# Unread products in the idle places of TensorE, two values in places of their own, and one copy moved to ScalarE

## The chip, the cores and the metric

The kernel runs on one core of a Trainium2 chip. The metric is the device time of one execution in microseconds (us); the time before is 784.37 us, the median of three runs (783.34 to 786.42). The core's engines work side by side, each through its own queue of instructions in order: TensorE (PE, with its weight loads shown as PEld) multiplies matrices into PSUM, VectorE (DVE) and ScalarE (ACT) work element by element, GpSimd (POOL) too, and SyncE (SP) issues transfers.

## The reference

A Perceiver of two layers: 128 latent rows of 256 numbers (`x`) attend to 12544 context rows. Each layer is cross attention to the context, a recurrent attention and a mixture of experts, each added to `x` after a layer norm (the last layer's, which the change touches, are the lines below). All is float32.

```python
x = x + L0_xattn(layernorm(x), ctx_1024, mask, ...)
x = x + L0_attn(layernorm(x), ...)          # gated delta net
x = x + L0_ffn(layernorm(x), ...)           # best expert of 8
x = x + L1_xattn(layernorm(x), ctx_1024, ...)
x = x + L1_attn(layernorm(x), ...)          # here
x = x + L1_ffn(layernorm(x), ...)           # and here

# L1_attn: 16 heads of 16
q, k, v = split(x @ Wqkv.T)
q, k = elu(q) + 1, elu(k) + 1
decay = sigmoid(decay_param)                # one for each head
running_kv   = scan(k * v, decay)           # out[t] = decay * out[t-1] + in[t]
running_ksum = scan(k, decay)
den = clip(sum(q * running_ksum, per head), 1e-6)
out = q * running_kv / den
g = sigmoid(out @ Wgate.T + bgate)
return (g * out + (1 - g) * v) @ Wout.T

# L1_ffn: the two best of 8 experts
gate = softmax(x @ Wg + bg); keep the two largest, normalised
y = x @ We + be for every expert; sum over experts weighted by gate
```

## The kernel before

Until about 744 us the kernel streams the context: for each block of 512 rows it makes keys and values, then scores, exponentials and weighted sums, first for layer 0 and then for layer 1, with the layers between filled in. The end of that is `weigh1`: the last weighted sums (L1084), copies of the sums to SBUF by ScalarE (L1107), four transposes into the PSUM tile `pt` (L1110), the division (L1113, L1117), the residual (L1121), and a copy of the row totals, `total`, out of `pt` by ScalarE (L1123).

Then `last_layers` computes the second layer's recurrent attention and experts for all 128 rows at once, with nothing left to stream; its weights are in SBUF by then. Here the order of TensorE, ScalarE and VectorE is the order in which the code calls them (`tc.manual_schedule`), and only data that is not there yet, or a place that is still being read or written, makes an instruction wait. In this function the steps are:

- `root` (L1306 on): mean and variance of `x` (L1309, L1310), the inverse root by Ln and Exp on ScalarE (L1312, L1313), `x` less its mean (L1316).
- Layer norm and transposition in one product with a scaled identity, `dg` (L1325, L1329); the result `hT` is copied to SBUF in two halves, by VectorE (L1330) and ScalarE (L1331).
- Keys, queries and values, transposed, as `pk`, `pq`, `pv` (L1337, two halves of the channels, two products each), and the residual `x` started in `po` (L1341).
- exp and relu of keys and queries (L1346 to L1349) and a copy of `v` (L1350) on ScalarE, then a load of the table for sigmoid (L1351); `min(exp, 1) + relu` and the scan of the keys on VectorE (L1354, L1355), the queries' (L1356), and their product (L1357).
- Denominators: a product that sums per head (`pd`, L1361), clipped, inverted (L1366, L1367), spread to 256 columns (`dx`, L1369) and transposed (`pr`, L1372). TensorE adds `v` through the output weights to `po` (L1377) while VectorE scans keys times values (L1379), multiplies by the queries (L1380) and by `pr` to give `o` (L1382).
- The gate: four products of `o` (`pg`, L1386), sigmoid (L1390), and the table for Ln and Exp (L1393). Since g*o + (1-g)*v = v + g*(o-v), VectorE takes `o - v` (L1394), works out whether all totals are in range (L1398 to L1400), and multiplies by the gate (L1402); TensorE adds the result through the output weights to `po` (L1403).
- The layer norm again (its transposes L1414), the router's logits `pl` (L1421), the eight experts' products `py` (L1425, L1455), the choice of two on VectorE (L1433 to L1449), and the weighted sum of the experts into `y_out` (L1469, L1476), which is written out.

Intermediate values lie in places of the context's buffers that are free by then, handed out one after the other by `room` and `both`; in the profile they are all called `ctx`. [...]

A second copy of the network, for totals out of range, stands behind a branch that these inputs do not take.

## Time and profile before

| | |
|---|---|
| median of three runs | 784.37 us |
| profiled execution, its time | 784.51 us |
| its span, first to last instruction | 782.6 us |
| mean granted TensorE clock | 0.992 of full speed |
| TensorE busy in the span | 749.9 us (96%) |
| the span from 744 us on | 38.6 us, TensorE busy 23.3, granted clock 0.83 |
| last product of weigh1's sums, last sum into y_out | 745.3, 776.7 us |

How to read it: the granted clock is the share of full speed that TensorE was given in a stretch; a product of float32 operands shows as two rows or more of matmul, each with a weight load, and rows overlap, so the time that one adds is the distance from start to start rather than its own duration. In the timeline the brackets give the idle time of the engine ahead of an instruction, and what ended it.

### The profile page before, as it was taken

The numbers are of one execution on the slowest core, as the hardware profiler recorded it, in microseconds if no ns is written. First come the engines' busy times: TensorE is split into PE (matmuls) and PEld (weight loads), VectorE is DVE, ScalarE is ACT, GpSimd is POOL, SyncE is SP. The second block draws the span as 40 slices with busy tenths as digits, with TensorE's granted clock in tenths as the row PEclk, the third lists the DMA queues.
The fourth block names the chain that finished last, engine by engine and source line by source line (L and its number), as shares of the span: only waits on it lengthen the run. The fifth ranks groups of instructions, "written<-read, shape, count | busy, mean of one in ns | idle before, by whom it ended". The sixth has DMA issues, their size and how long they took to land.

```text
span 782.6 us, 23795 instructions
## 1 busy us (share of the span) xinstructions
PE 749.9 (96%) x10821; PEld 558.0 (71%) x10821; DVE 250.5 (32%) x406; ACT 411.2 (53%) x540; POOL 246.4 (31%) x193
## 2 busy tenths in 40 slices
PE   4999999999999999999999999999999999999965
PEld 2667777777777776756668756667888888888852
DVE  0465445654466453983113133000000000000044
ACT  2244334433443334474224533336999999999940
POOL 6597677666776630416012011000000000000000
PEclk9999999999999999999999999999999999999988
DMA  9584000000000002233111345221442222222000
GB/s 291 213 280 172 9 8 4 8 8 8 7 6 6 2 15 84 85 117 123 58 44 41 106 128 134 78 81 58 121 115 74 68 58 74 68 58 72 4 1 12
DMA packets 35742, 56.70 MB, mean 72 GB/s; under 512 B 5760, under 2 KB 11952, under 8 KB 35632
## 3 DMA queue, kind: packets, MB, share of 16 engines
q1 hardware_dynamic: 35232, 54.00, 21.7%
q8 instruction: 87, 1.43, 0.8%
q0 software_dynamic: 400, 1.09, 0.5%
q14 instruction: 23, 0.19, 0.1%
HBM read 42.09 MB, written 12.98 MB: 70 GB/s over the span
## 4 chain that ended last, share of the span: by engine, by line
PE 90%; DVE 3%; ACT 2%; POOL 1%; issue 1%; DMA 1%; SPq 0%; ACTq 0%; DVEq 0%; POOLq 0%
PE st L1067 14%; PE ot L1084 12%; PE pk L395 11%; PE pv L1016 10%; PE pv L408 10%; PE pk L995 10%; PE st L437 6%; PE ot L455 6%; DVE acc L612 1%; DMA ctx<-in_ctxT 1%; POOL shift L428 1%; PE pr L602 1%; PE py L924 1%; PE py L1425 1%; PE pg L732 1%
## 5 line engine op out<-in xcount | busy, mean ns | idle before, releaser
L1073 ACT ACTIVATE e<-st 128x512 f32<-128x512 f32 x196 | 189.7, 1021 | 17.1 <-PE st L1067 15.7
L428 POOL TENSOR_TENSOR shift<-mb,nm 128x1024 f32<-128x1024 f32 x49 | 120.7, 2464 | 73.7 <-DVE e L443 59.3
L1067 PE MATMUL st<-qs,ks 32*128 32x128 f32 x3136 | 115.8, 283 | 0.8 <-ACT e L1073 0.8
L1067 PEld LDWEIGHTS st<-qs,ks 32*128 32x128 f32 x3136 | 96.9, 186 | 21.4 <-ACT e L1073 20.9
L444 ACT ACTIVATE e<-e 128x1024 f32<-128x1024 f32 x49 | 51.8, 1057 | 101.5 <-DVE e L443 100.0
L1084 PE MATMUL ot<-e,ctx 128*17 128x128 f32 x3136 | 104.7, 274 | 0.0
L395 PE MATMUL pk<-ctx,wkv 128*128 128x512 f32 (+1 forms) x200 | 93.7, 613 | 9.3 <-DMA ctx<-in_ctxT 9.3
L443 DVE TENSOR_TENSOR e<-st,shift 128x1024 f32<-128x1024 f32 x49 | 57.9, 1220 | 113.5 <-PE st L437 105.2
L995 PE MATMUL pk<-ctx,wk 128*128 128x512 f32 (+1 forms) x200 | 92.8, 591 | 1.3 <-ACT ctx L1021 1.3
L1016 PE MATMUL pv<-wv,ctx 128*128 128x256 f32 x392 | 92.8, 382 | 0.9 <-ACT kh L1002 0.9
L408 PE MATMUL pv<-wkv,ctx 128*128 128x256 f32 x392 | 89.2, 380 | 1.6 <-ACT kT L399 1.6
L408 PEld LDWEIGHTS pv<-wkv,ctx 128*128 128x128 f32 x392 | 74.2, 190 | 22.3 <-issue 10.0
L445 DVE TENSOR_TENSOR sums<-sums,e 128x1024 f32<-128x1024 f32 x49 | 87.8, 1792 | 4.8 <-ACT e L444 1.2
L1016 PEld LDWEIGHTS pv<-wv,ctx 128*128 128x128 f32 x392 | 72.8, 190 | 20.4 <-issue 10.0
L1084 PEld LDWEIGHTS ot<-e,ctx 128*17 128x17 f32 x3136 | 77.5, 97 | 11.9 <-ACT e L1073 0.3
L423 POOL TENSOR_SCALAR mb<-msk 128x256 f32<-128x256 uint8 x49 | 72.2, 1474 | 4.2
L395 PEld LDWEIGHTS pk<-ctx,wkv 128*128 128x128 f32 x200 | 37.1, 195 | 48.4 <-issue 45.4
L1113 DVE RECIPROCAL den<-pt 128x16 f32<-128x16 f32 x1 | 0.3, 257 | 208.7 <-PE pt L1110 208.7
L1002 ACT ACTIVATE kh<-pk,col 128x512 f32<-128x512 f32 (+1 forms) x50 | 33.9, 678 | 59.0 <-PE pk L995 58.8
L995 PEld LDWEIGHTS pk<-ctx,wk 128*128 128x128 f32 x200 | 36.1, 190 | 31.5 <-issue 26.5
L1021 ACT COPY ctx<-pv 128x512 f32<-128x512 f32 x49 | 28.7, 587 | 54.3 <-PE pv L1016 54.2
L412 ACT COPY v<-pv 128x512 f32<-128x512 f32 x49 | 28.6, 586 | 54.3 <-PE pv L408 54.3
(322 smaller groups left out, 620.3 us busy)
## 6 DMA issues: line engine op xcount, KB each, us to landing
ctx<-in_ctxT SPq DMA_DIRECT2D x24, 512.0 KB, 8.4
kd<-kh SPq DMA_DIRECT2D x48, 256.0 KB, 2.0
ks<-kd SPq DMA_DIRECT2D x192, 64.0 KB, 2.8
w<-in_L_ffn_expert_w SPq DMA_DIRECT2D x4, 512.0 KB, 3.7
ctx<-in_L_ffn_We SPq DMA_DIRECT2D x4, 512.0 KB, 4.7
msk<-in_maskT SPq DMA_DIRECT2D x24, 64.0 KB, 1.9
w<-in_L_attn_Wqk SPq DMA_DIRECT2D x2, 768.0 KB, 9.7
w<-in_L_attn_Wv SPq DMA_DIRECT2D x2, 768.0 KB, 5.1
```

The lines of the kernel that those rows point to most:

```text
L395: nc.tensor.matmul(pk[:, :n], wkv[:, k, m * 128 : (m + 1) * 128], ctx_blocks[b][:, k, :], start=(k == 0), stop=(k == KC - 1),)
L408: nc.tensor.matmul(pv[:, c, :], ctx_blocks[b][:, k, rows], wkv[:, k, D:], start=(k == 0), stop=(k == KC - 1),)
L423: nc.gpsimd.tensor_scalar(mb, msk[:, c0 * 128 : (c0 + 2) * 128].rearrange("p (c s) -> p c s", c=2), BIG, BIG, ALU.mult, ALU.subtract,)
L428: nc.gpsimd.tensor_add(shift, mb.unsqueeze(1).to_broadcast([128, 4, 2, S]), nm.unsqueeze(2).to_broadcast([128, 4, 2, S]),)
L443: nc.vector.tensor_add(e, st, shift)
L444: nc.scalar.activation(e, e, AF.Exp)
L445: nc.vector.tensor_add(sums, sums, e)
L995: nc.tensor.matmul(pk, wk1[:, k, m * 128 : (m + 1) * 128], ctx_blocks[b][:, k, :], start=(k == 0), stop=(k == KC - 1),)
L1016: nc.tensor.matmul(pv[:, c, :], ctx_blocks[b][:, k, rows], wv1[:, k, :], start=(k == 0), stop=(k == KC - 1),)
L1067: nc.tensor.matmul(st3[:, j - 1, g, :] if j else st1[:, 0, g, :], kss[b % 3][r, g // 2, g % 2, c * 128 : (c + 1) * 128], qs[r, g, :], star ...
L1073: nc.scalar.activation(e[:, j].rearrange("p j g s -> p (j g s)"), st.rearrange("p j g s -> p (j g s)"), AF.Exp,)
L1084: nc.tensor.matmul(ot[32 * j : 32 * j + DH + 1, g, :], v[:, c, 8 * (g // 2) + 2 * j + g % 2, :], e[:, j, g, :], start=False, stop=(i + 1 = ...
```

## The change

Within `last_layers` and nowhere else:

- A PSUM tile `spare` in a bank of its own, taken from `tl_a`, which goes from three banks to two; and a function `beat(n)`, which issues `n` products of the identity with 256 columns of the first weights into `spare`. Nothing reads `spare`. It is called five times: 7 ahead of the first layer norm, 1 after the residual, 2 ahead of the transposes of the denominators, 2 after the gate's products, and 2 after the last products into `po`.
- The keys' two halves go to two PSUM tiles, `pk0` and `pk1`, in place of one; `tl_y` then has four users (`pk0`, `pk1`, `pq`, `pv`) for its four places.
- The copy that spreads the denominators, `dx`, goes from VectorE to ScalarE, and the load of sigmoid's table from ahead of it to behind it.
- `o - v` is written to a new place, `away`, in place of over `o`.

```diff
-            tc.tile_pool(name="tl_a", bufs=3, space=PSUM) as ps_a,
+            tc.tile_pool(name="tl_a", bufs=2, space=PSUM) as ps_a,
...
+            spare = ps_o.tile([128, 512], F32, name="spare")
+
+            def beat(n):
+
+                for _ in range(n):
+                    nc.tensor.matmul(spare[:, :D], ident, wqkv[:, 0, :D], start=True, stop=True)
...
             po = ps_o.tile([128, 512], F32, name="po")
+            beat(7)
             xm, y0, t = root(x)
...
-            pk, pq, pv = [wide(f"p{n}").rearrange("p j (k s) -> p j k s", s=S)[:, 0] for n in "kqv"]
-            for dst, n in ((pk, 1), (pq, 0), (pv, 2)):
+            pk = [wide(f"pk{m}")[:, 0, :S] for m in range(KC)]
+            pq, pv = [wide(f"p{n}").rearrange("p j (k s) -> p j k s", s=S)[:, 0] for n in "qv"]
+            for dst, n in ((pk, 1), ((pq[:, 0], pq[:, 1]), 0), ((pv[:, 0], pv[:, 1]), 2)):
...
-                            dst[:, m, :], wqkv[:, k, c : c + 128], hT[:, k, :],
+                            dst[m], wqkv[:, k, c : c + 128], hT[:, k, :],
...
             nc.tensor.matmul(po[:, :D], ident, x, start=True, stop=False)
+            beat(1)
...
-                nc.scalar.activation(ek[:, m, :], pk[:, m, :], AF.Exp)
-                nc.scalar.activation(rk[:, m, :], pk[:, m, :], AF.Relu)
+                nc.scalar.activation(ek[:, m, :], pk[m], AF.Exp)
+                nc.scalar.activation(rk[:, m, :], pk[m], AF.Relu)
...
             nc.scalar.copy(v, pv)
-            nc.scalar.preload_act_table_set("sigmoid_and_others")
...
-            nc.vector.tensor_copy(dx, den.unsqueeze(2).to_broadcast([S, 16, 16]))
+            nc.scalar.copy(dx, den.unsqueeze(2).to_broadcast([S, 16, 16]))
+            nc.scalar.preload_act_table_set("sigmoid_and_others")
+            beat(2)
...
             nc.scalar.preload_act_table_set("natural_log_exp_and_others")
-            nc.vector.tensor_sub(o, o, v)
+            beat(2)
+            away = both()
+            nc.vector.tensor_sub(away, o, v)
...
-                nc.vector.tensor_mul(gate[:, m, :], gate[:, m, :], o[:, m, :])
+                nc.vector.tensor_mul(gate[:, m, :], gate[:, m, :], away[:, m, :])
                 nc.tensor.matmul(po[:, :D], gate[:, m, :], wgo[:, m, D:], start=False, stop=(m == KC - 1))
             x = po[:, :D]
+            beat(2)
```

## The prediction

> **What bounds the kernel now.** First the page: what sets the end, by engine.

> ```profile
> PE 90%; DVE 3%; ACT 2%; POOL 1%; issue 1%; DMA 1%; SPq 0%; ACTq 0%; DVEq 0%; POOLq 0%
> ```

> TensorE sets the end for 90% of the span, but the change touches only the last layers, from 746.7 us on. So I read that stretch in windows (columns: PE, PEld, DVE, ACT, POOL busy, then granted clock, DMA share, GB/s).

> ```profile
> 740.00:744.00 4.00, 4.00 (x134) 3.60 (x130) 0.00 (x0) 3.67 (x5) 0.00 (x0) 1.00 0.00 0
> 748.00:751.00 3.00, 0.77 (x3) 0.80 (x4) 1.73 (x7) 0.50 (x2) 0.00 (x0) 0.72 0.00 0
> 752.00:753.00 1.00, 1.00 (x6) 1.00 (x6) 0.00 (x0) 0.00 (x0) 0.00 (x0) 0.50 0.00 0
> 757.00:758.00 1.00, 0.45 (x5) 0.35 (x4) 0.87 (x4) 0.98 (x1) 0.00 (x0) 1.00 0.00 0
> 767.00:768.00 1.00, 1.00 (x2) 0.45 (x2) 0.78 (x5) 0.02 (x1) 0.00 (x0) 0.50 0.00 0
> 770.00:772.00 2.00, 2.00 (x6) 0.95 (x5) 1.29 (x3) 0.00 (x0) 0.00 (x0) 1.00 0.00 0
> ```

> ```profile
> 42.80:46.22 3.41, 1.79 (x9) 1.00 0.25 38
> 745.95:749.36 3.41, 0.71 (x4) 0.99 0.00 0
> 749.36:752.78 3.41, 2.54 (x10) 0.50 0.00 0
> 759.60:763.02 3.41, 1.89 (x12) 1.00 0.00 0
> 763.02:766.43 3.41, 1.64 (x10) 0.99 0.00 0
> ```

> After 0.71 and 1.64 us of work the clock fell, after 1.79 and 1.89 it stayed; a half-clock period with 2.54 did not bring it back, a full one did. Then the timeline of that stretch for who waits for whom (start, duration, instruction, idle before and its releaser):

> ```profile
> 747.58 0.17 ACT L1123 COPY total<-pt 128x16 f32<-128x16 f32 x1 [1.40 <-DVE x_xattn L1117]
> 750.23 1.20 PE L1329 MATMUL ln_pt<-ctx 128*128 128x128 f32 x4 [3.56 <-DVE ctx L1325]
> 753.25 1.91 PE L1337 MATMUL pq<-ctx,w 128*128 128x128 f32 x8
> 757.98 0.29 DVE L1369 COPY ctx<-ctx 128x256 f32<-128x256 f32 x1
> 759.96 1.16 PE L1386 MATMUL pg<-ctx,w 128*128 128x128 f32 x8 [0.32 <-DVE ctx L1382]
> 761.15 0.43 DVE L1394 TENSOR_TENSOR ctx<-ctx,ctx 128x256 f32<-128x256 f32 x1 [1.25 <-PE pg L1386]
> 762.32 1.13 PE L1403 MATMUL po<-w,ctx 128*128 128x256 f32 x4 [1.20 <-DVE ctx L1402]
> 763.49 0.43 DVE L1309 BATCH_NORM_STATS2 ctx<-po 128x6 f32<-128x256 f32 x1 [1.02 <-PE po L1403]
> ```

> A product is two passes in these rows (L1377 has two products and four passes). Pass to pass, 128 columns take 0.11 us at full clock (pg) and 0.213 at half (pq); 256 columns take 0.217 (L1377, 1.03 for four) and so about 0.43 at half (py's 512 columns step 0.43 at full, 0.85 at half).

> **The change, part by part.** *Seven unread products at the head.* The spare bank is the one that pt had; the first product waits for the copy to total, which ends at 747.75. They run from 747.79: 14 passes x 0.217 = 3.04, to 750.83 at full clock. The real product, queued behind them on TensorE, could start at 750.23: 0.60 late. What this buys, if the clock holds: ln_pt's first result at 751.2, copy by VectorE 0.29, keys from 751.57 (751.38 before); 16 passes of keys and queries at 0.11, so pq is there at 753.50 (755.17 before). From pq to the denominators' product it takes 1.66 as now (ScalarE 0.68, VectorE 0.42 and 0.42, handoffs): 755.16 in place of 756.83. **Gain 1.7.** If it falls amid the seven, say at 748.5: 1.7 of them at full clock, then four until the next edge at 751.9, the rest by 752.5; keys from 753.2 at full clock, denominators at 756.75: gain 0.1. Bounds: 1.7 and, wholly at half clock, a loss (rival three). I take 1.7; the choice hangs on one period. The one that ended at 749.36 would hold 0.71 + 1.57 = 2.28 us, above the 1.79 that kept the clock. [...]

> *Keys' halves in places of their own.* ScalarE may start after four passes, not eight. At half clock queries end last anyway (scan done at 755.37, eq and rq at 755.87), gain 0. At full clock it keeps the second scan at 754.1, beside rq, where one tile would make it 754.4: contained in the 1.7. Four wide banks hold four users, and the narrow pool going from 3 to 2 adds no wait: each reused bank's reader (pd, pr, pg, ln_pt, pl) is already an ancestor of the next writer.

> *One unread product after po*: 0.43. At full clock TensorE ends pv at 754.21, po 754.64, this 755.07; the denominators' product is ready at 755.16. Hidden by 0.09; at half clock po and it would cost up to 1.6.

> *Spreading copy to ScalarE.* VectorE loses 0.295 + 0.02 before its scans. On ScalarE I take 0.38 (v's copy, 128x256, took 0.37; the bounds are 0.30 and that), so pr starts 0.08 later, 0.45 after the reciprocal, and ends at 0.89; scans and product take VectorE to 1.17. Hidden by 0.28, with the two unread products (0.87) done at 0.1. The 1.28 table load now stands behind this copy; it ends 0.8 before the sigmoid's data. **Gain 0.30.**

> *Difference to a place of its own.* L1394 overwrote pg's operand and so waited until pg had ended; now it runs straight after o, hidden by pg, with the three total checks (0.56). From pg's start: the second sigmoid ends at 1.56 as now, the second gate product at 1.84. TensorE ends pg at 0.88, two unread products at 1.75, then po's four passes: 1.75 + 3 x 0.217 + 0.38 = 2.78, statistics at 2.80 against 763.49 - 759.96 = 3.53. **Gain 0.73**; without the unread ones it would be 0.98, so they cost 0.25 here.

> *Two unread products after po*: 0.87, behind them a transpose that starts 1.38 after the statistics; hidden by 0.6. They put about 2.5 us of work into every period across this place (least 2.1 without transposes), above 1.79. [...] VectorE then bounds: from the statistics, router done at 6.24, six expert sums x 0.52 to 9.46, the flag's two operations behind TensorE's pw and ScalarE's copy, next sum at 10.08, then 0.52 + 0.49 + 0.09 + 0.42 to 11.60, against 776.68 - 763.49 = 13.19. **Gain 1.6.**

> Sum: 1.7 + 0.30 + 0.73 + 1.6 = 4.3 off the profiled execution's 784.51 us (span 782.6): **780.2**. That execution is 0.14 over the median 784.37, so 0.53% faster.

> **Rivals.** *One half-clock stretch stays.* [...] The first stays: 0.1 + 0.30 + 0.73 + 1.6 = 2.7, 781.8. The second stays: also 2.7, 781.8. *The unread products don't hold the clock*, both stay: 0.1 + 0.30 + 0.73 = 1.1, 783.4. Against: unread or not, they are products of full size.

> *Slower: the seven stand in the way at half clock.* The queue is in order; should the clock be low from 747.8 and stay so, they take 14 x 0.43 = 6.0, to 753.8; projections as now put the denominators 3.6 late, the product after po adds up to 1.6, and 1.0 comes back further on: 784.51 + 4.2 = 788.7. It decides from the point where TensorE comes free of the seven after 752.8 with the clock still at half up to the denominators (the other gains, 2.6, are then gone). Against: the seven fill a period, and a full period brought the clock back.

> **How the numbers follow.** Both hold 0.50; one stretch stays 0.35 (the first 0.30); both stay 0.07; slower 0.08. The likeliest gives 780.2, its own range 778.8 to 781.6 (the timed runs before spread over 3.1). 778.7 to 783.8 leaves out the slower case and a tenth at both edges. A measurement of this kernel tells about 0.5%, 3.9 us, from no change: 780.45. Faster: 0.44 of the 0.50, as the sum lies near that line but runs of the kernel before with other edges lose more at half clock, and 0.04 of the next case: 0.48. Slower 0.08; the same 0.44.

> **What would show it.** Right: granted clock 1.00 from 749 to 757 and from 766 to 770; ln_pt at about 750.9, denominators 1.7 earlier; pr released by ScalarE; the difference inside pg; y_out bound by VectorE. Wrong: 0.50 over the unread products themselves, ln_pt later than 752, or half clock in py all the same.

## The result

Median 780.89 us (779.75 to 783.62, eight runs) against 784.77 for the kernel before (783.34 to 786.65, eight runs): a ratio of 0.9951 with a 95% interval of 0.9933 to 0.9968, that is 3.9 us or 0.5% faster. The profiled execution took 779.82 us, its span 777.5.

The page's chain by engine hardly moves (TensorE 91% of the span, 90% before), as the stretch in question is only 3% of it.

The windows of the changed kernel over the places that ran at half clock before (columns as in the prediction; the last line is the whole stretch, from the first transpose into `pt` to the end of the last sum into `y_out`):

```profile
747.00:750.00 3.00, 3.00 (x15) 2.64 (x15) 1.73 (x7) 0.50 (x2) 0.00 (x0) 1.00 0.00 0
751.00:752.00 1.00, 1.00 (x11) 1.00 (x10) 0.07 (x1) 0.55 (x3) 0.00 (x0) 1.00 0.00 0
764.00:766.00 2.00, 2.00 (x6) 0.95 (x5) 1.61 (x10) 0.00 (x0) 0.00 (x0) 1.00 0.00 0
744.96:771.61 26.65, 23.41 (x114) 16.75 (x114) 18.43 (x65) 8.38 (x23) 0.00 (x0) 1.00 0.00 1
```

TensorE has full clock all through. The stretch took 26.65 us; before, from 745.96 to 776.68, it took 30.72. These 4.07 us are what the change did in this pair of executions. The other 1.0 us of the difference between the two spans is not its doing: it is the time of the first transpose, which stood anywhere between 744.7 and 749.3 in the profiles of this study, though nothing ahead of it is changed in any experiment but two (e4 and e8 put one product there). So I compare kernels by the stretch, in parts, each read from one profiled execution. The timelines give the borders, first of the kernel before, then of the changed one:

```profile
745.96 0.71 PE L1110 MATMUL pt<-ident,oTs 128*128 128x128 f32 x4 [0.62 <-ACT oTs L1107]
756.86 0.59 PE L1361 MATMUL pd<-ctx,ctx 128*128 128x8 f32 x4
766.08 7.09 PE L1425 MATMUL py<-ctx,ctx 128*128 128x512 f32 x12
776.26 0.42 DVE L1476 TENSOR_TENSOR y_out<-y_out,pb 128x256 f32<-128x256 f32 x1
```
```profile
744.96 0.71 PE L1110 MATMUL pt<-ident,oTs 128*128 128x128 f32 x4 [0.62 <-ACT oTs L1107]
746.81 3.29 PE L1325 MATMUL spare<-w,ident 128*128 128x256 f32 x14 [1.13 <-ACT total L1123]
749.93 0.61 PE L1337 MATMUL ln_pt<-ctx 128*128 128x128 f32 x4
754.42 0.61 PE L1370 MATMUL pd<-ctx,ctx 128*128 128x8 f32 x4
756.07 0.20 PEld L1383 LDWEIGHTS pr<-ident,ctx 128*128 128x128 f32 x2 [0.48 <-ACT ctx L1378]
757.14 0.42 DVE L1407 TENSOR_TENSOR ctx<-ctx,ctx 128x256 f32<-128x256 f32 x1
757.22 1.11 PE L1397 MATMUL pg<-ctx,w 128*128 128x128 f32 x8
760.09 0.43 DVE L1309 BATCH_NORM_STATS2 ctx<-po 128x6 f32<-128x256 f32 x1 [1.04 <-PE po L1416]
762.70 5.40 PE L1439 MATMUL py<-ctx,ctx 128*128 128x512 f32 x12
771.19 0.42 DVE L1490 TENSOR_TENSOR y_out<-y_out,pb 128x256 f32<-128x256 f32 x1
```

The seven unread products start when the copy of the totals is done (the trace puts 1.13 us of TensorE's idle time ahead of them down to that copy); `ln_pt` follows them with no wait of its own. `pr` is released by ScalarE's copy; `o - v` (L1407) runs beside `pg`; the experts' twelve passes take 5.40 us in place of 7.09.

| part, from and to | before | after | gain | predicted |
|---|---|---|---|---|
| head: first transpose to `pd` | 10.90 | 9.46 | 1.44 | 1.7 |
| spread: `pd` to `pg` | 3.10 | 2.80 | 0.30 | 0.30 |
| gate: `pg` to the statistics | 3.53 | 2.87 | 0.66 | 0.73 |
| experts: statistics to the end | 13.19 | 11.52 | 1.67 | 1.6 |
| sum | 30.72 | 26.65 | 4.07 | 4.3 |

### The profile page after: what moved, and what is told of

Its sections match the earlier page's. It is cut to its first block, busy times and chain, and to the rows that moved or that the text cites. A ratio compares the mean times of both kernels' runs of the same rounds, so it can differ in the third digit from the quotient of the medians.

```text
span 777.5 us, 23850 instructions
## 1 busy us (share of the span) xinstructions
PE 750.1 (96%) x10849; PEld 559.4 (72%) x10849; DVE 250.3 (32%) x405; ACT 411.5 (53%) x541; POOL 246.3 (32%) x193
## 4 chain that ended last, share of the span: by engine, by line
PE 91%; DVE 2%; ACT 2%; POOL 1%; issue 1%; DMA 1%; SPq 0%; ACTq 0%; POOLq 0%; DVEq 0%
PE st L1067 14%; PE ot L1084 12%; PE pk L395 11%; PE pv L1016 10%; PE pv L408 10%; PE pk L995 10%; PE st L437 6%; PE ot L455 6%; DVE acc L612 1%; POOL shift L428 1%; DMA ctx<-in_ctxT 1%; PE pr L602 1%; PE py L924 1%; PE pg L732 1%; PE py L1439 1%
## 5 line engine op out<-in xcount | busy, mean ns | idle before, releaser
L995 PEld LDWEIGHTS pk<-ctx,wk 128*128 128x128 f32 x200 | 36.1, 190 | 31.6 <-issue 26.5
```

What stands on the lines that cost most here:

```text
L995: nc.tensor.matmul(pk, wk1[:, k, m * 128 : (m + 1) * 128], ctx_blocks[b][:, k, :], start=(k == 0), stop=(k == KC - 1),)
```

## Experiments

Theory one: most of the gain is TensorE's clock, which the unread products hold up. Theory two: it is the shorter chain between VectorE and ScalarE, and the products do nothing. Beside these, three questions: do transposes hold the clock as products do, does the head's queue cost what was reckoned, and does the clock's fall go with long idle gaps or with little busy time in a period. The times of e1 to e4 were taken beside one series of the kernel before (median 785.52, thirteen runs), those of the others beside another (784.97, 23 runs).

**The products alone (e1) and the edits alone (e2).** e1 keeps `beat` and its calls and undoes the rest; e2 is the reverse; `tl_a` has two banks in both. The main lines of e1 against the changed kernel:

```diff
-            pk = [wide(f"pk{m}")[:, 0, :S] for m in range(KC)]
-            pq, pv = [wide(f"p{n}").rearrange("p j (k s) -> p j k s", s=S)[:, 0] for n in "qv"]
+            pk, pq, pv = [wide(f"p{n}").rearrange("p j (k s) -> p j k s", s=S)[:, 0] for n in "kqv"]
...
+            nc.scalar.preload_act_table_set("sigmoid_and_others")
...
-            nc.scalar.copy(dx, den.unsqueeze(2).to_broadcast([S, 16, 16]))
-            nc.scalar.preload_act_table_set("sigmoid_and_others")
+            nc.vector.tensor_copy(dx, den.unsqueeze(2).to_broadcast([S, 16, 16]))
...
-            away = both()
-            nc.vector.tensor_sub(away, o, v)
+            nc.vector.tensor_sub(o, o, v)
```

e2 drops `spare`, `beat` and its five calls; its first lines against the changed kernel:

```diff
-            spare = ps_o.tile([128, 512], F32, name="spare")
...
-            beat(7)
```

> Unread products alone; the difference, the keys' places and the spreading copy as before. Measured from the first transpose into pt to the end of the last sum into y_out: 30.72 us in the kernel before, 26.65 in the changed one. Theory one (most of the gain is the clock held up): head 1.2 (the keys' split would add 0.26), spread 0, gate 0 (the difference waits for the gate's products as before), experts 1.6: 27.9, time about 2.8 under before. Theory two (the gain is the shorter chain between VectorE and ScalarE): 30.7, time as before.

> No unread product at all; the three other edits stay. Theory one: head 0 at half clock, spread 0.30, gate 0.98 (no unread products in the way), experts 0 with the clock fallen: 29.4 us for the same stretch, time 1.3 under before, and two half-clock periods in the stretch as before. Theory two: 26.7, time 3.9 under before.

Measured: e1 27.81 us for the stretch, median 781.31, ratio 0.9947 (0.9930 to 0.9963). e2 29.32 us, median 783.15, ratio 0.9969 (0.9958 to 0.9980). By parts, e1: head 9.64, spread 3.13, gate 3.52, experts 11.52; e2: head 10.69, spread 2.80, gate 2.62, experts 13.21. So the products bring 2.91 and the edits 1.40; together they bring 4.07 and not 4.31, for the two products after the gate take 0.25 of what the difference's own place gives (2.62 without them, 2.87 with). Theory two falls. By their times e1 (780.52 to 781.48) and e2 (782.08 to 784.11) are apart, but e1 is not told from the changed kernel; what the edits add to the products is read from the profiles alone. e1's head shows the keys' split: 9.64 against 9.46, 0.18, and that at full clock. In e2 the clock fell in the head, and there VectorE sits idle for 0.99 until the queries are there, so the keys' earlier values are not what it lacks; that its head is 0.21 shorter than before goes with a clock that came back 8.70 after the first transpose in place of 10.19. First `py` of e1 at full clock, then from the timeline of e2 the half clock again:

```profile
763.60 5.40 PE L1437 MATMUL py<-ctx,ctx 128*128 128x512 f32 x12
```
```profile
752.03 2.08 PE L1338 MATMUL pk<-ctx,w 128*128 128x128 f32 x8
756.36 0.42 DVE L1356 SCALAR_TENSOR_TENSOR ctx<-ctx 128x256 f32<-128x256 f32 x1 [0.99 <-ACT ctx L1350]
765.33 7.09 PE L1427 MATMUL py<-ctx,ctx 128*128 128x512 f32 x12
```

**Transposes for products (e3).**

```diff
-            beat(7)
+            for _ in range(26):
+                nc.tensor.transpose(spare[:, :128], wqkv[:, 0, :128], ident)
```

> The seven products at the head replaced by 26 transposes of 128 columns of the same weights into the same spare bank, about 2.9 us of TensorE at full clock. [...] If they count as any other work: full clock, 26.5 to 27 us.

Measured: 26.42 us, `ln_pt` at 4.74 after the first transpose, clock full; mean clock 0.997 in three executions and 0.995 in one; median 780.37, ratio 0.9938 (0.9917 to 0.9958). One period of its trace (length, busy time of TensorE with its count of rows, clock; the periods' ends, the edges, are laid 3.41 us apart from the steps of the clock in the same trace) and the timeline over it:

```profile
747.19:750.61 3.42, 2.64 (x24) 1.00 0.00 0
```
```profile
746.12 0.71 PE L1110 MATMUL pt<-ident,oTs 128*128 128x128 f32 x4 [0.62 <-ACT oTs L1107]
747.97 3.06 PE L1330 MATMUL spare<-ident,w 128*128 128x128 f32 x26 [1.13 <-ACT total L1123]
```

All of this period's work is transposes (one row each, where a product shows two), and the clock stayed at 1.00 after it, while in the kernel before it fell after 0.71 us of them. So these 2.64 us of float32 transposes kept the clock as the seven products do.

**The head's products where they need not wait (e4).** In `weigh1`, into a bank for scores:

```diff
+            st = ps_st.tile([128, 3, G, S], F32, tag="st3", name="early", bufs=2)
+            st = st.rearrange("p j g s -> p (j g s)")[:, :D]
+
+            def early(n):
+                for _ in range(n if loaded else 0):
+                    nc.tensor.matmul(st, ident, w1[0][:, 0, :D], start=True, stop=True)
+
+            early(1)
             for g in range(G):
                 nc.tensor.transpose(pt[:, g * 128 : (g + 1) * 128], oT[:, g, :], ident)
+            early(8)
...
-            beat(7)
```

> The head's products issued in the function before, into a score bank that is free by then: one ahead of the transposes into pt, eight behind them, so they don't wait for the copy of the totals, and TensorE is free at about 4.1 us after the first transpose, when the norm's scaled identity is ready. Queue theory (the seven stood 0.6 us in the way): ln_pt at 4.3 us after the first transpose instead of 4.97, stretch 26.0. Clock: no gap of more than 0.3 us is left at the head, so no half-clock period there in any execution, mean clock 0.998 in all; median 0.5 to 1.2 us under the changed kernel's, that is about 4.7 under before. If the end is set elsewhere: no difference to the changed kernel.

Measured, from its timeline:

```profile
746.86 0.71 PE L1118 MATMUL pt<-ident,oTs 128*128 128x128 f32 x4
751.14 0.68 PE L1345 MATMUL ln_pt<-ctx 128*128 128x128 f32 x4
```

`ln_pt` came at 4.28 in place of 4.97, `pd` at 8.84 in place of 9.46, the stretch 26.03; median 780.11, ratio 0.9929 (0.9912 to 0.9945); mean clock 0.997 or 0.998 in all four executions. The queue theory holds to 0.03 us.

**Fourteen products at the head (e7).**

```diff
-            beat(7)
+            beat(14)
```

> Fourteen unread products at the head in place of seven: 28 passes of 0.217 from 1.85 us after the first transpose. Queue theory: the norm's product starts 3.04 us later than in the changed kernel, at 8.0 after the first transpose in place of 4.97, and everything behind it with it: stretch 29.7, time about 3 over the changed kernel and 1 under before. If unread products gave way to real ones: 26.65. The clock stays at 1.00 over the head in most executions; where an edge near 748 to 749 finds too little work, the fourteen run at half clock and it is up to 3 us more.

Measured: median 784.92, ratio 0.9993 (0.9980 to 1.0007): all that the change brings is gone. In the profiled execution the clock fell at 748.34, amid the fourteen, so `ln_pt` came 9.68 after the first transpose and the stretch took 31.35, longer than before:

```profile
748.16 8.00 PE L1325 MATMUL spare<-w,ident 128*128 128x256 f32 x28 [1.13 <-ACT total L1123]
756.00 0.61 PE L1337 MATMUL ln_pt<-ctx 128*128 128x128 f32 x4
```

Of the twelve executions, the eight with a mean clock of 0.997 or 0.998 took 782.56 to 786.27 (median 783.79, some 3.5 over those of the changed kernel with such a clock in the same series); the four with 0.995 took 786.03 to 786.53. The fourteen did not give way to the real product: `ln_pt` stands behind all 28 of their rows.

**Without the last two (e6).**

```diff
             x = po[:, :D]
-            beat(2)
```

> The changed kernel without the two unread products after the last products into po; all others stay. [...] Share of a period: between the end of po and the experts a period can hold as little as 1.4 to 1.8 us of work, around the 1.64 that lost and the 1.79 that kept the clock, so it falls in some executions and not in others: then 1.7 to 3 us longer, 28.3 to 29.6, and a mean clock 0.0022 to 0.0044 lower in part of the runs; median 0.5 to 2 us over the changed kernel's.

Measured: 28.34 us, the experts' part 13.22 as in the kernel before, the other parts as in the changed kernel; median 783.09, ratio 0.9967 (0.9947 to 0.9987); mean clock 0.994 to 0.996 in all six executions, where the changed kernel's executions have either 0.995 or 0.997 to 0.999. I had expected the fall in some executions only; the mean clock of all six speaks for at least one half-clock period in each (one of 3.41 us takes 3.41 x 0.5 / 783 = 0.002 off the mean, an estimate), though only the profiled one shows where. By the times alone e6 is not told from the changed kernel (0.9955 in the same series, e9 below). Two of its periods, the second ending where the clock fell, and the gap ahead of the experts:

```profile
747.68:751.10 3.42, 1.71 (x34) 1.00 0.00 0
764.75:768.16 3.41, 2.00 (x9) 1.00 0.00 0
```
```profile
765.80 0.41 PE L1427 MATMUL ln_pt<-ident,ctx 128*128 128x128 f32 x2 [1.41 <-DVE ctx L1316]
767.03 7.09 PE L1438 MATMUL py<-ctx,ctx 128*128 128x512 f32 x12
```

The longest gap that reaches into the second is the 1.41 us ahead of `ln_pt`, and the clock fell: no longer one was needed here. But busy time in the period doesn't settle it alone either: it fell after 2.00 and stayed after 1.71.

**The changed kernel again (e9).**

> The changed kernel again, beside the others on one chip. Free-running edges: its executions fall in two groups, mean clock 0.998 and 0.995, the second 1.5 to 2.5 us longer, with some third of them in the second; median 3.9 to 4.5 under before.

Measured: median 781.76, ratio 0.9955 (0.9940 to 0.9970): 3.2 under before, less than expected, with half of the executions in the second group in place of a third. Mean clock 0.995 in four executions (781.85, 782.24, 782.51, 783.50) and 0.997 or 0.998 in the other four (779.43 to 781.68). The profiled one was of the first four and shows what the prediction had drawn as its first rival:

```profile
743.91:747.33 3.42, 1.66 (x35) 1.00 0.00 0
747.33:750.74 3.41, 3.41 (x8) 0.50 0.00 0
```
```profile
747.24 4.97 PE L1325 MATMUL spare<-w,ident 128*128 128x256 f32 x14 [1.13 <-ACT total L1123]
752.05 0.61 PE L1337 MATMUL ln_pt<-ctx 128*128 128x128 f32 x4
```

The edge lay 0.09 us into the seven; they took 4.97 in place of 3.29, the full period brought the clock back at 750.74, and `pd` came 11.14 after the first transpose: 0.24 later than before. The rest of the stretch is as in the other profile (2.80, 2.87, 11.52), 28.33 in all.

**A leaner version (e8).** This is e4 with one product after the gate in place of two and none after the residual:

```diff
             nc.tensor.matmul(po[:, :D], ident, x, start=True, stop=False)
-            beat(1)
...
             nc.scalar.preload_act_table_set("natural_log_exp_and_others")
-            beat(2)
+            beat(1)
```

> As e4_early, and one unread product after the gate in place of two, none after the residual. The pair after the gate held po back by 0.25 and the one after the residual the denominators by about 0.1. Stretch from the first transpose into pt: 26.03 - 0.2 - 0.1 = 25.7, if one product after the gate still leaves every period over 1.8 us of work; median 0.3 under e4_early, 1.2 under the changed kernel. If the clock falls before the experts: 1.7 longer in some executions.

Measured: 25.78 us, median 779.57 (778.95 to 781.18), ratio 0.9936 (0.9921 to 0.9950), beside the changed kernel's 0.9955 in the same series; mean clock 0.997 or 0.998 in all six. By parts: head 8.84 (as e4, so the product after the residual had cost nothing), gate 2.63 in place of 2.87, experts 11.52. Its head, from the timeline:

```profile
745.84 3.62 PE L1114 MATMUL early<-w,ident 128*128 128x256 f32 x16
749.57 0.68 PE L1345 MATMUL ln_pt<-ctx 128*128 128x128 f32 x4
```

Its median lies under those of the kernel before and of the changed one, but the intervals of e8 and e9 overlap: what it gains over the changed kernel is shown by the stretch (25.78 against 26.65), and e4 and e8 are not told apart by their times.

## Why the prediction was right, point by point

The likeliest case gave 780.2 us, the median is 780.89, the likeliest case's own range held it. Its mechanism is the one that ran: the clock held in both places in the profiled execution, the four parts came out at 1.44, 0.30, 0.66 and 1.67, and e1 and e2 show that most of it is the clock. That the first median lies so near the sum is in part luck: three of its eight executions have the lower mean clock, in e9 four of eight, and there the gain was 3.2.

*The head* was mis-sized by 0.26. The seven took 3.12 us from the first to `ln_pt`'s start, not 3.04, and `pk` came 0.13 later than reckoned (5.74 after the first transpose; 751.57 was 5.61). The other half came between `pk` and `pd`, 3.72 in place of 3.59: I stepped the keys' passes at 0.11 from the first on, while their second product waits for ScalarE's half of `hT`, which landed at 750.85 with the first pass at 750.70.

*If the clock falls amid the seven*: I put this at a gain of 0.1; e9 shows a loss of 0.24, since the edge came earlier (0.09 us into the seven, 0.71 in the case that I worked out), and more of the seven ran at half clock.

*Edges that stand elsewhere in another run*: the 0.30 that I put on the head's half clock, and the runs of the kernel before "with other edges" in the chance of faster, take this for granted; no trace of before shows it, and no run shows what the edges go by. What the runs show: in the first profile a period ends 1.45 us after the first transpose (eight steps of 3.41 back from the clock's fall at 773.72), holds 2.00 us of work, and the clock stayed; in e9 one ends 1.94 after it, holds 1.66, and the clock fell. The mean clock of the kernel before goes from 0.988 to 0.992, with 0.992 in the profiled execution. 7 of the 16 executions of the changed kernel have the mean clock of 0.995. The seven have a median of 782.24, the other nine 780.47: 1.8 apart, where the stretches of e9 and of the first profile differ by 1.68 (28.33 - 26.65). So the median gain is a mixture of cases and not the 4.07 of one pair of profiles. But the clock does not fix an execution's time: in the first eight the fastest (779.75) has 0.995 and the slowest (783.62) 0.999.

*The transposes* are 0.71 of the 2.28 us of work for which I took the head's clock to hold. e3 bears this out: a period with 2.64 us of them and nothing else kept it.

*Gaps or share*: to go by the busy time of a period, and not by the length of a gap, was right: without the last two products the clock fell after a gap of no more than 1.41 us (e6). A line of busy time between the 1.64 us after which it fell and the 1.79 after which it stayed, before, fits all periods but one. With the periods laid at each trace's own clock steps, the clock fell after 1.66 (e9) and stayed after 1.71 (e6) and 1.75 (e1), and at the end of e6 it fell after 1.71; that puts it at about 1.7, an estimate from these traces and for them alone. The one against it is the 2.00 after which it fell in e6: 0.46 of that are the router's products alone, of eight columns each, and without them it is 1.54. Whether they hold the clock less than wider ones was not shown.

*Gate*: 0.66 against 0.73, po's first pass at 1.80 after `pg` in place of 1.75; that its two products cost 0.25 is shown by e2 and e8. *Spread* was right to 0.01: `pr` started 0.55 after the reciprocal and not 0.45, but ScalarE's copy (0.40) stayed hidden behind VectorE's scans, as did the table load behind it. *Experts*: right within 0.07.

*The slower rival* needed half clock from the first product to the denominators. No profile shows it: a period of 3.41 us of work at half clock brought the clock back each time (e9, e7). But e7 shows the queue that it was made of: with twice the products the whole gain is gone.

## What to carry to other kernels

Where a chain of small products alternates with other engines, read the granted clock in the windows first: here half clock in the next dense stretch cost more than the chain's waits (2.91 us against 1.40), and unread products in the idle places bought it back. They stand in the queue where the next real product is ready first (e7: with seven more, `ln_pt` 9.68 us after the first transpose in place of 4.97), so put them where nothing is ready, make them end just before the next real product is ready, and choose their output place so that they can start when the gap starts (e4: `ln_pt` at 4.28). Where executions of one kernel differ in their mean clock (here 0.995 and 0.997 to 0.999), one profile shows one of several outcomes; look at the mean clock of every execution.

## What was not expected

- With the 1.13 us of waiting for the totals' copy ahead of the seven (746.81), 7 of 16 executions have the mean clock of 0.995; with the wait filled (e4, e8) none of ten was under 0.997.
- Twenty-six transposes and seven products of 256 columns held the clock alike in the profiled executions (26.42 and 26.65 us for the stretch).
- A half-clock period with 2.54 us of work in it (749.36 to 752.78, before) did not bring the clock back, while at full clock 1.71 was enough to keep it once (e6).
